# Two token tiles of a query unit share one double PSUM buffer during the query fill

## The chip, the cores and the metric

The kernel runs on one core of a Trainium2 chip. The metric is the device time of one execution in microseconds. The core's engines work side by side, each through its own queue in order: TensorE (PE, matmuls, with weight loads shown as PEld), VectorE (DVE), ScalarE (ACT), GpSimd (POOL), and SyncE (SP), which here issues every DMA. Matmul results land in PSUM, a memory of eight banks; a bank holds 512 fp32 values on each of 128 partitions.

## The reference, cut to what matters

The input x has 8 sequences of 1024 tokens with 512 features. It is normalised, and then a Performer attention block with its own MLP, and an RWKV-like feed-forward block, both work on the normalised tokens; the output is the sum of x and of both.

```python
def _phi(u, omega):
    proj = jnp.einsum('bhsk,mk->bhsm', u, omega)          # 16 heads, k = 32, m = 128
    sq = 0.5 * jnp.sum(u * u, axis=-1, keepdims=True)
    stab = jnp.max(proj, axis=-1, keepdims=True)
    return jnp.exp(proj - sq - stab) / jnp.sqrt(m) + 1e-06
...
pq = _phi(q * scale, omega)
pk = _phi(k * scale, omega)
kv = jnp.einsum('bhsm,bhsk->bhmk', pk, v)
z = jnp.sum(pk, axis=2)
num = jnp.einsum('bhsm,bhmk->bhsk', pq, kv)
den = jnp.einsum('bhsm,bhm->bhs', pq, z)
out = num / den[..., None]
h = out.transpose(0, 2, 1, 3).reshape(B, S, H * K) @ wo
...
x = layernorm(x + h);  x = layernorm(x + gelu(x @ w1 + b1) @ w2 + b2)
```

The change touches how `_phi` is computed for the queries: the products with omega, their maximum and their exponentials.

## The kernel before, in words

**Precision.** Each fp32 matrix is split into a high and a low fp16 half, and a product is made of three fp16 matmuls (`mm3`, line 139): 12 matmuls for one 128 x 512 result.

**Stages.** First the keys, values and the feed-forward block (to some 1000 us), then the queries, the attention output and the MLP. The second part runs over 64 units; a unit `(b, u)` is 512 tokens (half a sequence) times 4 heads. For each unit, one after another over neighbouring slots:

- `proj_a` (line 413) projects the queries (tile psu), ACT and DVE split the result into u, and SP stores it (ud) and transposes it. `proj_l` (line 455) loads it back as skq; `norm` (line 437) makes the squares.
- `QB` (line 631), once for each of four tiles of 128 tokens: four matmuls write the products with omega, one for each head, into a PSUM buffer pj; DVE takes the maximum (mxq) and makes the bias (biq); ACT takes four exponentials into e and casts the high half (eq); the low half is subtracted on POOL for tiles 0 and 2 and on DVE for tiles 1 and 3; SP transposes the pair into pq.
- `QD` (line 659), twice, for tiles 0 and 1 and for tiles 2 and 3: 24 matmuls with pq into acn, then three DVE steps (nm, rc, ot). `QE` (line 692) splits and transposes the result (oT).
- `O` (line 762) multiplies with wo for each 128 tokens (tile pso); `pre` (line 790) does the layer norm and SP transposes its result into x1b; `mlp1` and `mlp2` (psw, acc) are the MLP.

**The order.** Every step is put on a time axis with `at(tau, ...)`, and the program is written in the order of tau; the axis runs in units of one slot. Matmuls are chained in that order (`mm`, line 136), so PE's queue is fixed by it. The other queues are chained as well, except between tau 72.55 and 81.55: `unpin` (line 878) removes their chains and `tail_banks` (line 146) sets them again. In that stretch a planner of the framework orders ACT, DVE, POOL and SP by when their inputs are ready in its own model, and by the order of writing among those that are ready.

This stretch is the query fill. Units 0 to 7 have their QB there, one unit in each slot. `QF` (line 57) and `QDF` (line 56) place the steps of a slot: tile 0 of the unit at 0.10, tile 1 at 0.30, the first half of QD of the unit before at 0.45, tile 2 at 0.52, QD's second half at 0.75, the projection of the next unit at 0.86, tile 3 at 0.90. So tile 3 stands directly ahead of tile 0 of the next unit, with no other matmul between them unless feed-forward matmuls are placed there. Those (psk, psr, psf) are spread over the fill up to about 78.2; the O steps of block 0 stand in slots 6.5 and 6.8 after the fill's start.

**The buffers.** `open_p` (line 115) opens the PSUM pool of pj with two buffers of shape 128 x 2 x 4 x 128, two banks each, as the key stage writes two tiles at a time. `QB` takes one such buffer for each tile and uses its first half. A buffer is given out again when all that used it is done. After `tail_banks` the pool is another one (pS), with two buffers of one bank.

In the profile most rows name line 137 (the matmul helper) or line 185 (the helper of the other engines), so rows are told apart by their tiles.

Of the kernel before, what the change touches and what calls it, by code (L numbers as in the profile page):

```python
# [60 lines left out]
def block_kernel(ctx, tc, x, wq, wk, wv, wo, om3, ln1_g, ln1_b, w1, b1, w2, b2,  # L61
# [74 lines left out]
    def mm(*a, **k):  # L136
        return chained("pe", nc.tensor.matmul(*a, **k))  # L137
# [24 lines left out]
    def st(shape, dt, name, bufs=2, tag=None):  # L162
        tag = tag or name
        pool = pools["k"] if tag in KPOOL else pools["c"] if tag in CPOOL else pools["q"] if tag in QPOOL else sp
        return pool.tile(shape, dt, name=name, tag=tag, bufs=bufs)
# [4 lines left out]
    def pst(name, k):  # L170
        pool, tag, shape = P[k]
        return pool.tile(shape, F32, name=name, tag=tag)
# [49 lines left out]
    def Y(j, t):  # L222
        return 0 if j is None else (warp(j, t),)
# [404 lines left out]
        spq.dma_start(out=ff_d[bk * 4 + t], in_=r)  # L628


    def QB(b, u, t, j=None):
        if t == 0:
            qst[b, u] = []
        p = (19.12, 21.9, 24.68, 27.46)[t]
        sk, nsq = stk["q", b, u], nrm["q", b, u]
        e = st([128, 4, 128], F32, "e", 4)
        pj = pst("pj", "pj")[:, 0]
        for h in range(4):
            mm(pj[:, h, :], sk[:, h, t * 128:(t + 1) * 128], oms, start=True, stop=True)
        yield Y(j, p + 0.3)  # L640
        mx = st([128, 4], F32, "mxq", 4)
        dve.tensor_reduce(mx, pj, AX.X, ALU.max)
        yield Y(j, p + 1.05)
        bi = st([128, 4], F32, "biq", 4)
        dve.scalar_tensor_tensor(bi, mx, -1.0 / (SU * SU), nsq[:, t * 4:t * 4 + 4], ALU.mult, ALU.add)
        yield Y(j, p + 1.3)
        for h in range(4):
            act.activation(e[:, h, :], pj[:, h, :], AF.Exp, bias=bi[:, h:h + 1], scale=1.0 / (SU * SU))
        eq = st([128, 2, 4, 128], F16, "eq", 3)
        act.copy(eq[:, 0], e)  # L650
        yield Y(j, p + (3.9 if t == 0 else 3.1))
        eng = dve if QLO[t] == "v" else gps
        eng.tensor_tensor(eq[:, 1], e, eq[:, 0], ALU.subtract)
        yield Y(j, p + (5.3 if t == 0 else 4.2))
        pq = st([128, 2, 4, 128], F16, "pq", 4)
        spq.dma_start(out=pq, in_=eq.rearrange("p z h m -> p (z h) m"), transpose=True)
        qst[b, u].append(pq)
# [237 lines left out]
    for i in range(NU):  # L895
        b, u = divmod(i, 8)
# [42 lines left out]
    for i in range(NU):  # L939
        b, u = divmod(i, 8)  # L940
# [16 lines left out]
        for t in range(4):  # L957
            if j + 1 < 0:
                at(s + 1 + QF[t], QB, b, u, t)
            else:  # L960
                at(warp(j + 1, (19.12, 21.9, 24.68, 27.46)[t]), QB, b, u, t, j + 1)
# [140 lines left out]
```

## Time and profile before

| | |
|---|---|
| median of 5 runs | 2952.76 us (2950.97 to 2957.46) |
| the profiled execution, its own time | 2950.67 us |
| its span in the profile | 2948.6 us |
| PE busy | 2781.7 us (94%) |
| DVE busy | 2260.8 us (77%) |
| ACT busy | 1758.6 us (60%) |
| POOL busy | 1018.2 us (35%) |
| first and last QB matmul of the fill | 1006.44 and 1162.55 us |
| maximum of a query tile on DVE (mxq) | 0.69 us each |
| exponential of a tile and head on ACT (e) | 0.37 us each |
| landing of a pq transpose, 1100 to 1170 us | 3.2 us |

A row of the timeline holds the start, the length, the engine, the line, the operation, the tile written, the tiles read, and the number of instructions merged into the row; in brackets stands the idle time before it and what ended that. Rows of one queue overlap where the engine pipelines. A wait for several inputs is put down to the one that came last. In the table of windows each engine has its busy time and, in brackets, its number of instructions.

### The profile page before, as it was taken

Reading aid. Unit: us, or ns where it says so; the run is one execution under the profiler, and the core shown is the slowest. Engines: PE = TensorE matmul, PEld = TensorE weight load, DVE = VectorE, ACT = ScalarE, POOL = GpSimd, SP = SyncE. Lnnn points to the kernel's source line nnn. Section 1 sums busy time; section 2 is a strip of 40 time slices with the busy share of each in tenths; the row PEclk is TensorE's granted clock in tenths of the full one; section 3 lists DMA queues with packets and bytes.
Section 4 is the critical chain, followed back from the end, with each engine's and each line's share of the span. In section 5 each row is a group of like instructions: output and inputs, shape, how many; then the busy total and the mean of one; then the engine's idle time right before and its main releaser. Section 6 shows DMA issues by size and latency. Waiting matters only on the chain. (4 is left out here: it accounts for less than half of the span.)

```text
span 2948.6 us, 52107 instructions
## 1 busy us (share of the span) xinstructions
PE 2781.7 (94%) x18784; PEld 1389.2 (47%) x18784; DVE 2260.8 (77%) x4312; ACT 1758.6 (60%) x3888; POOL 1018.2 (35%) x941
## 2 busy tenths in 40 slices
PE   4999999999998896999999999999999999999996
PEld 2554445455454443444444444444444444444442
DVE  6897888889788666667778778778777777778654
ACT  5888988888888464555555455455455454554210
POOL 3464555555543432222223223223223232232111
PEclk8999999999999997999999999999999999999998
DMA  7666667666664368868777777778777777776432
GB/s 204 158 183 172 181 169 185 187 180 181 175 168 125 116 156 198 191 149 190 173 175 176 180 174 171 189 165 177 181 167 175 183 171 172 178 176 155 118 100 86
DMA packets 839348, 494.81 MB, mean 168 GB/s; under 512 B 632017, under 2 KB 718129, under 8 KB 837041
## 3 DMA queue, kind: packets, MB, share of 16 engines
q1 hardware_dynamic: 839088, 491.49, 67.0%
q8 instruction: 147, 2.41, 0.4%
q14 instruction: 113, 0.92, 0.1%
HBM read 226.95 MB, written 113.38 MB: 115 GB/s over the span
## 5 line engine op out<-in xcount | busy, mean ns | idle before, releaser
L137 PE MATMUL psw<-x1b,w1s 128*128 128x512 f16 x3072 | 695.4, 380 | 0.8 <-DVE u L185 0.8
L137 PE MATMUL acc<-w2h,gg 128*128 128x512 f16 x2048 | 647.8, 379 | 0.0
L137 PEld LDWEIGHTS <-w1s 128*128 128x128 f16 x3072 | 296.4, 98 | 344.5 <-issue 3.4
L137 PEld LDWEIGHTS <-gg 128*128 128x128 f16 x3072 | 292.8, 98 | 324.0
L185 ACT ACTIVATE g<-psw,b1t 128x512 f32<-128x512 f32 x256 | 172.6, 686 | 371.7 <-PE psw L137 362.3
L185 ACT ACTIVATE e<-pj,biq 128x128 f32<-128x128 f32 x1024 | 291.6, 369 | 162.0 <-DVE biq L185 138.3
L137 PE MATMUL acc<-w2l,gg 128*128 128x512 f16 x1024 | 387.8, 379 | 0.0
L185 ACT ACTIVATE e<-pj,bik 128x128 f32<-128x128 f32 x1024 | 287.4, 397 | 41.5 <-DVE bik L185 41.4
L185 POOL TENSOR_TENSOR eq<-e,eq 128x512 f16<-128x512 f32 x128 | 164.7, 1286 | 387.8 <-ACT eq L185 242.7
L185 DVE TENSOR_REDUCE mxq<-pj 128x4 f32<-128x512 f32 x256 | 175.7, 687 | 108.3 <-PE pj L137 107.3
L185 POOL TENSOR_TENSOR u<-ot,u 128x512 f16<-128x512 f32 x64 | 84.3, 1318 | 470.7 <-ACT u L185 431.8
L185 ACT ACTIVATE u<-psu 128x512 f16<-128x512 f32 x128 | 76.4, 597 | 206.0 <-PE psu L137 203.2
L185 DVE SCALAR_TENSOR_TENSOR gg<-g,gg 128x512 f16<-128x512 f32 x256 | 188.1, 735 | 8.8
L185 DVE TENSOR_SCALAR gg<-g 128x512 f16<-128x512 f32 x256 | 107.9, 421 | 106.7 <-ACT g L185 106.7
L137 PE MATMUL psv<-whv,xb 128*128 128x512 f16 x512 | 167.4, 389 | 19.9 <-DMA xb<-u 18.3
L185 POOL TENSOR_TENSOR e<-u 128x512 f32<-128x512 f16 x128 | 162.3, 1268 | 69.1 <-DMA u<-u 62.6
L137 PE MATMUL psu<-xb,whk 128*128 128x512 f16 x512 | 156.9, 389 | 27.3 <-DVE v L185 23.3
L185 ACT ACT_TABLE_LOAD x114 | 146.3, 1283 | 58.0 <-DVE biq L185 48.7
L185 POOL TENSOR_TENSOR xf<-xf,be 128x512 f32<-128x512 f32 x64 | 81.5, 1273 | 287.7 <-DMA xf<-in_x 168.8
L185 DVE SCALAR_TENSOR_TENSOR ekl<-e,ekh 128x1024 f16<-128x1024 f32 x128 | 171.6, 1341 | 5.1 <-ACT ekh L185 4.9
L137 PE MATMUL psf<-whfv,kx 128*128 128x512 f16 x512 | 162.5, 379 | 7.2 <-DVE v L185 2.8
L185 ACT CAST eq<-e 128x512 f16<-128x512 f32 x256 | 158.6, 621 | 16.4 <-DMA pq<-eq 9.0
(163 smaller groups left out, 5721.6 us busy)
## 6 DMA issues: line engine op xcount, KB each, us to landing
w1s<-w1d SPq DMA_DIRECT2D x256, 256.0 KB, 3.0
ud<-u SPq DMA_DIRECT2D x128, 256.0 KB, 2.2
skk<-ud SPq DMA_DIRECT2D x192, 128.0 KB, 2.8
skq<-ud SPq DMA_DIRECT2D x192, 128.0 KB, 3.2
xt<-in_x SPq DMA_DIRECT2D x64, 256.0 KB, 3.3
xnd<-xt SPq DMA_DIRECT2D x64, 256.0 KB, 2.5
xtd<-xb SPq DMA_DIRECT2D x16, 1024.0 KB, 5.3
ffd<-rsg SPq DMA_DIRECT2D x64, 256.0 KB, 2.7
```

The source lines that it names most:

```text
L137: return chained("pe", nc.tensor.matmul(*a, **k))
L185: return lambda *a, **k: chained(self.key, f(*a, **k))
```

## The change

In the fill, an even tile takes a double buffer, uses its first half and leaves the second half for the odd tile that follows. The odd tile takes that half instead of a new buffer. So tiles 0 and 1 share one buffer and tiles 2 and 3 share the other. After the fill, where a buffer has one bank only, every tile takes its own as before. The order of the program is not edited.

```diff
+    pjh = {}
+
     def QB(b, u, t, j=None):
         if t == 0:
             qst[b, u] = []
         p = (19.12, 21.9, 24.68, 27.46)[t]
         sk, nsq = stk["q", b, u], nrm["q", b, u]
         e = st([128, 4, 128], F32, "e", 4)
-        pj = pst("pj", "pj")[:, 0]
+        if t % 2 and (b, u) in pjh:
+            pj = pjh.pop((b, u))
+        else:
+            two = pst("pj", "pj")
+            pj = two[:, 0]
+            if two.shape[1] == 2:
+                pjh[b, u] = two[:, 1]
         for h in range(4):
             mm(pj[:, h, :], sk[:, h, t * 128:(t + 1) * 128], oms, start=True, stop=True)
```

## The prediction

> **What bounds the kernel now.** I read the page first: the span, the busy slices, the clock row. The tensor engine (PE) is busy 94% of the span, so only the places where it is not busy can give time back.
>
> ```profile
> span 2948.6 us, 52107 instructions
> ...
> PEclk8999999999999997999999999999999999999998
> ```
>
> The clock has one dip inside the run, in slice 16. So I split the span at the fill of the query stage. Columns: length, busy time and instructions of PE, weight load, DVE, ACT and POOL, then granted clock, DMA share, GB/s.
>
> ```profile
> 1006.00:1102.80 96.80, 94.04 (x653) 47.05 (x654) 58.22 (x111) 61.96 (x149) 33.93 (x29) 0.98 0.64 152
> 1102.80:1163.00 60.20, 28.38 (x270) 16.18 (x269) 43.53 (x99) 27.11 (x74) 20.00 (x17) 0.75 0.84 191
> 1163.00:2948.60 1785.60, 1747.61 (x11158) 855.34 (x11155) 1327.80 (x2819) 841.13 (x1722) 448.66 (x350) 0.99 0.70 166
> ```
>
> The first query tile is written at 1006.44. Up to 1102.8 the fill is dense, because FFN matmuls stand between the tiles. From 1102.8 to 1163.0 they have run out: PE is idle 60.20 - 28.38 = 31.8 us, at a clock of 0.75. After 1163.0 PE is 98% busy, so whatever moves 1163.0 moves the end. The waits of PE from 1100 to 1165 (total, times, longest):
>
> ```profile
> PE pj L137 <- ACT e L185: 17.3, 3, 7.9
> PE acn L137 <- DMA pq<-eq: 12.1, 3, 7.0
> ```
>
> The first row is what the change works on: a tile's products wait for a bank whose exponentials are not done. It is 0.59% of the span. The second row is the next wait down the same queue. The PE timeline of the last of the three rounds shows how the two lie:
>
> ```profile
> 1144.41 0.61 PE L137 MATMUL pj<-oms,skq 96*128 96x128 f16 x8
> 1152.91 0.58 PE L137 MATMUL pj<-oms,skq 96*128 96x128 f16 x4 [7.89 <-ACT e L185]
> 1153.29 0.89 PE L137 MATMUL acn<-zq,pq 128*128 128x33 f16 x24
> 1154.02 0.59 PE L137 MATMUL pj<-oms,skq 96*128 96x128 f16 x4
> 1154.70 0.50 PE L137 MATMUL acn<-zq,pq 128*128 128x33 f16 x12
> 1162.19 0.52 PE L137 MATMUL acn<-zq,pq 128*128 128x33 f16 x12 [6.98 <-DMA pq<-eq]
> 1162.55 0.59 PE L137 MATMUL pj<-oms,skq 96*128 96x128 f16 x4
> ```
>
> By the issue order of the code the eight matmuls at 1144.41 are tile 3 of unit 6 and tile 0 of unit 7; 1152.91 is tile 1, which takes the buffer that tile 3 has just filled. Then come the first half of QD of unit 6, tile 2 (1154.02), and the second half of that QD, whose last twelve matmuls wait until 1162.19 for the transposed features of **tile 3 of unit 6**, the very tile written at 1144.41. Where that latency goes, first DVE and then the SP queue:
>
> ```profile
> 1148.10 1.25 DVE L185 TENSOR_TENSOR ot<-nm,rc 128x256 f32<-128x256 f32 x1
> 1149.27 1.27 DVE L185 TENSOR_REDUCE mxq<-pj 128x4 f32<-128x512 f32 x2
> 1150.53 0.69 DVE L185 SCALAR_TENSOR_TENSOR u<-psu,u 128x512 f16<-128x512 f32 x1
> 1151.14 0.54 DVE L185 SCALAR_TENSOR_TENSOR biq<-mxq,nsqq 128x4 f32<-128x4 f32 x2
> 1153.53 0.69 DVE L185 TENSOR_REDUCE mxq<-pj 128x4 f32<-128x512 f32 x1 [1.85 <-PE pj L137]
> 1154.64 0.69 DVE L185 TENSOR_TENSOR eq<-e,eq 128x512 f16<-128x512 f32 x1
> ```
>
> ```profile
> 1153.16 0.53 SPq L185 DMA_DIRECT2D ud<-u  x1
> 1157.45 1.25 SPq L185 DMA_DIRECT2D skq<-ud  x3
> 1158.81 6.53 SPq L185 DMA_TRANSPOSE pq<-eq  x4
> ```
>
> Tile 3's maxima start at 1149.27 only, 4.25 us after its matmuls ended, because DVE has been busy without a gap since 1124.07 with the layer norm of block 0. Its low part is ready at 1155.33 (1154.64 + 0.69), but its transpose stands on SP behind the loads of skq, which wait for ud to land: 1158.81. It lands and PE goes on at 1162.19. None of these steps asks when tile 1 was written.
>
> **The change part by part.** Removed instructions: none. Added: none; the pick of the half is done while the program is written out. In the fill 8 units x 4 tiles took 32 buffers by turns, and now take 16. After the fill the buffer is one bank wide, the new branch isn't entered, and the order there is written out by hand: 0.
>
> *Tile 1 no longer waits for tile 3 of the unit before.* In the three rounds that wait is 3.25 (at 1106.62), 6.16 (at 1134.16) and 7.89 (at 1152.91): 17.3 us. *A wait is added at tile 2*: it now takes the double buffer in which tile 3 of the unit before stands, so it waits for the same exponentials. Behind it on PE stand the second half of QD, the projection of the next unit and tile 3; DVE's sums of that half wait for them. Round by round:
>
> Round 1. Tile 1 and QD (0.38 + 0.73 us to the next start) go ahead at 1103.4, and the nine O matmuls after them. The next step waits for the DMA of oT until 1113.44 before and after, as its transpose was issued at 1106.77 from a tile finished ahead of all this. So 1.71 grows to about 4.96 and the gain is 0. The long gap may cost clock. The row for that: after the 4.38 us gap that ended at 1006.44, the psr matmuls start 0.43 us apart instead of 0.22, for about eight of them, 1.7 us. Behind it lie 1.35 us of waiting for pq (until 1118.72) and 0.43 for DVE (until 1124.81), 1.78 together, which hide it; with that cover gone it costs 1.7.
>
> Round 2. Tile 1 goes from 1134.16 to about 1128.0, QD's first half to 1128.4; tile 2 waits for tile 3's exponentials until 1134.16, where before it came at 1135.27. The second half of QD still ends its wait when tile 3's transpose lands, at 1140.31: the wait of 3.82 grows by what is won. Gain 0.
>
> Round 3. Tile 1 goes at 1145.0. QD's first half then meets a wait of its own: the transpose of tile 1 of unit 6 was issued from 1146.39 on and takes some 3.2 us to land, so about 1149.6; tile 2 follows tile 3's exponentials at 1152.80 instead of 1154.02, and the end is 1162.19 as before. DVE's 1.85 us of idleness before 1153.53 goes, so tile 3's subtraction can come up to 0.29 earlier (its cast ends at 1154.35, it starts at 1154.64); the SP row at 1158.81, 3.5 us later, hides that. Gain 0.
>
> [...]
>
> *The order on DVE, ACT, POOL and SP.* Only PE is pinned between 72.55 and 81.55 on the code's time axis; the other four queues are ordered by a planner by the time at which work is ready in its own model, earlier-written work first. Tile 1's steps (a reduce and a bias on DVE, four exponentials and a cast on ACT, a subtraction on DVE, one transpose on SP, which may now pass the x1b and oT transposes and the w2 loads) become ready sooner, and QD's three DVE steps with them, so these orders can change from about 1102.8 on. The trace of before cannot show the new orders; the bounds come from its rows. Downwards: tile 3's transpose ahead of skq, 1158.81 - 1155.33 = 3.48 in round 3 and 1137.12 - 1136.54 = 0.58 in round 2; its maxima at once, 4.25 in round 3 and 1130.79 - 1128.00 = 2.79 in round 2; sum 11.1. Upwards: tile 1's maxima, bias and exponentials (0.69 + 0.15 + 1.14 = 1.98) and its transpose (1.24) put ahead of tile 3's, 3.22 a round, 9.7. A smaller unknown lies inside DVE's busy stretch: a step ot takes 0.42 alone but 1.25 at 1148.10, while POOL runs; such collisions can come or go at some 0.8 each. I take 0 for all this, the nearest row: written order puts tile 3's steps ahead of tile 1's, and DVE has the same work between 1124 and 1149 either way.
>
> Sum: 0 + 0 + 0 + 0. The profiled execution took 2950.67, its span of 2948.6 and 2.07 around it; the median shown is 2952.76, 2.09 higher. Forecast 2952.8.
>
> **The rivals.** *A, faster: the new orders shorten tile 3's way.* For it: tile 1's old lateness held SP back as well (its transpose could not be issued before 1146.39, after a subtraction at 1145.65). Against: the chain through DVE, ud and skq stands. Price: the SP parts and the maxima of round 2, 3.48 + 0.58 + 2.79 = 6.9, giving 2945.9; with all 11.1, 2941.7; the whole removed wait, 17.3, would give 2935.5.
>
> *B, slower: tile 1 is served ahead of tile 3.* Written three in a row, tile 1's reduce and exponentials can run while tile 3's cast or bias is not quite ready, and engines keep their order. Price 1.98 to 3.22 a round, 5.9 to 9.7 in all; in the middle 7.8, giving 2960.6. It decides from three full rounds on: with two it stays within 0.2%, about what a measurement of this kernel can tell from no change (5.9 us). Against: tile 3's steps are written first.
>
> *C, the change doesn't do what it says:* if the buffer were followed as a whole, tile 1 would wait for tile 0's exponentials, 1.1 us after tile 3's (a pair takes 2.17). Three rounds: up to 3.3 us, 2956.1. For it: the matmuls into kac at 964.44 wait for a read of other columns of the same bank. Against: here the halves are 512 fp32 values, a bank each.
>
> **How the numbers follow.** Forecast 0.49, A 0.24, B 0.21, C 0.06. Faster is A, 0.24; slower is B, 0.21; the forecast and C fall within 0.2%: 0.55. The range goes down to A's middle, 2944, and up to B's, 2961, which leaves out about half of A and of B, 2 in 10; the forecast alone lies in 2949 to 2957.
>
> **What would show it.** Right: tile 1 follows tile 0 on PE without a wait; the row of pj waiting for exponentials falls from 17.3 to about 7.4 (1129.1 to 1134.16 and 1150.4 to 1152.80) and stands at tile 2; acn waiting for pq grows; the first psw starts within 3 us of 1162.93; PE's idle time from 1102.8 on stays near 31.8. A shows as psw before 1157 with pq ahead of skq on SP; B as tile 3's cast behind tile 1's exponentials. The prediction fails if the orders differ enough to bring a wait on SP or ACT that no row here shows.

## The result, and the profile after

| | before | after |
|---|---|---|
| median | 2952.27 us (37 runs) | 2957.14 us (19 runs) |
| profiled span | 2948.6 us | 2955.3 us |
| from the first query tile to the first psw matmul | 156.49 us | 161.66 us |
| from there to the end of the span | 1785.67 us | 1786.07 us |

The changed kernel takes 1.0018 of the time of before, 95% interval 1.0012 to 1.0024: 4.9 us more. That is just inside the 0.2% that the forecast called no change, and yet clearly slower. The third row is worked out from the two timelines (1162.93 - 1006.44 and 1169.23 - 1007.57), the fourth from the spans. Of the 6.7 us between the two spans 5.2 lie in the query fill, 0.4 behind it, and 1.1 ahead of it, where the two programs are the same; the last section says how far figures from one profile carry.

The forecast said that tile 1 would follow tile 0 on PE without a wait. It does not. The same stretch of the PE timeline after the change, rounds 1, 2 and 3, starting each time with tile 3 of one unit and tile 0 of the next (x8), and the first psw row:

```profile
1107.13 0.61 PE L137 MATMUL pj<-oms,skq 96*128 96x128 f16 x8
1112.03 0.38 PE L137 MATMUL pj<-oms,skq 96*128 96x128 f16 x4 [4.29 <-ACT e L185]
...
1131.85 0.61 PE L137 MATMUL pj<-oms,skq 96*128 96x128 f16 x8
1143.15 0.58 PE L137 MATMUL pj<-oms,skq 96*128 96x128 f16 x4 [10.69 <-ACT e L185]
...
1156.51 0.91 PE L137 MATMUL pj<-oms,skq 96*128 96x128 f16 x8
1161.53 0.59 PE L137 MATMUL pj<-oms,skq 96*128 96x128 f16 x4 [4.12 <-ACT e L185]
...
1169.23 1.06 PE L137 MATMUL psw<-x1b,w1s 128*128 128x512 f16 x2
```

The exponentials of the pair on ACT, rounds 1 and 2:

```profile
1109.81 2.18 ACT L185 ACTIVATE e<-pj,biq 128x128 f32<-128x128 f32 x8 [1.44 <-DVE biq L185]
...
1140.94 2.16 ACT L185 ACTIVATE e<-pj,biq 128x128 f32<-128x128 f32 x8
```

Tile 1 starts at 1112.03 and 1143.15, when all eight exponentials are done (1109.81 + 2.18 = 1111.99; 1140.94 + 2.16 = 1143.10), so it waits for those of **tile 0**, the tile in the other half of its own buffer, and not for tile 3's, which end 1.1 us earlier. The list of the built program's PE queue says the same: in the fill every odd tile carries a wait on ACT, 16 of 16, and no even tile does. A pair from it:

```
14730 L137 Matmult pj_15277<-oms_266,skq_15016 128x128
14732 L137 Matmult pj_15277<-oms_266,skq_15016 128x128
14734 L137 Matmult pj_15277<-oms_266,skq_15016 128x128
14736 L137 Matmult pj_15277<-oms_266,skq_15016 128x128
14738 L137 Matmult pj_15277<-oms_266,skq_15016 128x128 [waits Activation_49]
```

The first four matmuls write tile 0's half of buffer 15277; the fifth, the first of tile 1, writes the other half and waits. The framework follows the buffer as one thing: a write to one half waits for the reads of the other.

That wait also stands in the dense part of the fill, where there was none before. PE and ACT after, unit 1:

```profile
1027.95 0.39 PE L137 MATMUL pj<-oms,skq 96*128 96x128 f16 x4
...
1034.91 0.58 PE L137 MATMUL pj<-oms,skq 96*128 96x128 f16 x4 [3.98 <-ACT e L185]
```

```profile
1031.76 0.63 ACT L185 ACTIVATE who<-wst 128x512 f16<-128x512 f32 x1 [1.27 <-DMA wst<-in_wo]
1032.30 1.03 ACT L185 CAST mx<-xm 128x1024 f16<-128x1024 f32 x1
1033.23 0.59 ACT L185 ACTIVATE kr<-psk 128x512 f32<-128x512 f32 x1
1033.72 1.13 ACT L185 ACTIVATE e<-pj,biq 128x128 f32<-128x128 f32 x4
```

Tile 0's exponentials stand on ACT behind the split of a weight (who) that is still being loaded, though DVE had their bias ready at 1029.26; tile 1 with all the FFN matmuls (of the feed-forward block) behind it waits 3.98 us for them. The waits of PE over the whole fill after the change, to be read beside the 17.3 and 12.1 of before:

```profile
PE pj L137 <- ACT e L185: 23.5, 5, 10.7
PE acn L137 <- DVE nm L185: 5.4, 2, 3.9
PE acn L137 <- DMA pq<-eq: 5.3, 3, 3.3
```

The wait that the change was to take away has grown by 6.2 us; the wait for the transposed features has shrunk by 6.8, and 5.4 of waiting for DVE are new.

### The profile page after: what moved, and what is told of

It is laid out like the page before. It is cut to its first block, busy times and chain, and to the rows that moved or that the text cites. A ratio compares the mean times of both kernels' runs of the same rounds, so it can differ in the third digit from the quotient of the medians.

```text
span 2955.3 us, 52123 instructions
## 1 busy us (share of the span) xinstructions
PE 2783.3 (94%) x18784; PEld 1389.9 (47%) x18784; DVE 2257.6 (76%) x4312; ACT 1762.1 (60%) x3888; POOL 1018.7 (34%) x941
## 5 line engine op out<-in xcount | busy, mean ns | idle before, releaser
L185 POOL TENSOR_TENSOR x<-x,bb 128x512 f32<-128x512 f32 x64 | 88.2, 1378 | 239.2 <-ACT u L185 165.6
```

What stands on the lines that cost most here:

```text
L185: return lambda *a, **k: chained(self.key, f(*a, **k))
```

## The experiments

Three theories. **W**: the loss is the wait of the odd tiles for the even tiles' exponentials, with the orders that the planner makes around it. **O**: the loss is a reordering of the other queues, above all DVE's in round 2, and a better order gives it back. **M** is the forecast's own claim, which the change as built could not test: even without any wait for a buffer the fill would not get shorter, as QD's wait takes over. The intervals of the ratios below reach some 0.09% to each side, 2.7 us (0.15% and more in the pair with the written order).

### Four buffers of one bank

```diff
     def open_q():
         early.close()
+        wide2.close()
+        ppq = proj.enter_context(tc.tile_pool(name="ppq", bufs=4, space=PSUM, side="right"))
+        P["pj"] = (ppq, "pj", [128, 1, 4, 128])
```

(`wide2` holds the pool with the two double buffers, which the key stage needs until then.)

> The key stage keeps its two double buffers; from the start of the query fill the products get four buffers of one bank, one for each tile, so that no tile waits for another tile of its own unit. Nothing is shared. If the loss of the change (+0.18%) comes from the wait of the odd tiles for the even tiles' exponentials, it is gone here: the waits of pj at 1034 and in the three rounds disappear or shrink below 3 us in all. Then the forecast's own theory is put to the test: the wait of QD for the transposed features of tile 3 takes over, and the time is that of before, 2949 to 2955 (ratio 0.999 to 1.001). If, against it, the 17.3 us of waiting were real gain: 2935 (0.994). If the loss came from tile 1 being ready sooner and the queues being reordered by that, this kernel is slower than before too, 2957 or more (1.0018).

Measured: ratio 0.9997, 0.9989 to 1.0006; median 2950.73. The waits of PE in its fill, and round 3:

```profile
PE acn L141 <- DMA pq<-eq: 16.2, 2, 9.5
PE acn L141 <- DVE nm L189: 7.8, 2, 5.0
PE pso L141 <- DMA oT<-u: 6.6, 1, 6.6
```

```profile
1144.37 0.83 PE L141 MATMUL pj<-oms,skq 96*128 96x128 f16 x12
1145.04 0.76 PE L141 MATMUL acn<-zq,pq 128*128 128x33 f16 x24
1145.65 0.38 PE L141 MATMUL pj<-oms,skq 96*128 96x128 f16 x4
1151.08 0.50 PE L141 MATMUL acn<-zq,pq 128*128 128x33 f16 x12 [5.05 <-DVE nm L189]
1158.23 0.52 PE L141 MATMUL acn<-zq,pq 128*128 128x33 f16 x12 [6.64 <-DMA pq<-eq]
```

Here four tiles do stand in a row: tile 3 of unit 6 and tiles 0 and 1 of unit 7 (x12), QD's first half, tile 2, none of them waiting. No wait of pj for exponentials is left in the fill. What took its place is 16.2 us of waiting for pq, 7.8 for DVE and 6.6 for oT. The first psw comes 155.73 us after the first query tile, against 156.49. So M holds, with the orders that the planner makes of the four buffers, which are not those of before: the whole 17.3 us of waiting can be taken away and 0.8 us of the fill is gained in this profile, less than the times can tell from nothing; their interval leaves room for 3.2 us at most.

### The change for the first four units alone, and for the last four alone

```diff
-            if two.shape[1] == 2:
+            if two.shape[1] == 2 and u < 4:      # the other run: u >= 4
```

> The change for units 0 to 3 alone, the dense part of the fill. By the two traces, the way from the first query tile to the first of the three rounds is 3.24 us longer with the change (96.32 before, 99.56 after), from a wait of 3.98 us of unit 1's tile 1 for unit 1's tile 0. If that wait does it, this kernel is slower by about 3 us, 2955.5 (1.001), and nothing is lost from 1103 on. If the loss is made by the orders in the three rounds, it is at 2952 (1.000).

> The change for units 4 to 7 alone. By the two traces the rest of the loss, 5.57 - 3.24 = 2.3 us, is made in the three rounds: 7.9 lost in round 2, where tile 3's maxima stand behind layer norm steps on DVE, and 5.8 won back. If the parts add up: 2954.5 (1.0008). If the loss is all in the dense part: 2952 (1.000). If the order in round 2 is what costs and nothing gives it back: 2957 to 2960.

Measured: first four 1.0000 (0.9990 to 1.0010), last four 1.0006 (0.9997 to 1.0016). Neither part is clear of no change, and the two sum to 0.0006 where the whole gave 0.0018; with intervals this wide that is no contradiction, but the split of the loss between the dense part and the rounds is not settled by the times. In the traces both have their waits: the first psw comes 158.80 us after the first query tile with the first four (2.3 later than before, with a wait of 3.83 in unit 1), and 160.64 with the last four (4.2 later, with a wait of 11.28 in round 2).

The traces settle more of the split than the times do. From the first query tile to round 1 the fill takes 99.56 to 101.48 us in the four profiles that have the wait there (the changed kernel, the first four, and two runs below: the wait alone, and the changed kernel with the norm behind the maxima), and 96.32 to 99.04 us in five that don't have it (the kernel before, the four buffers, the last four, and below the late load and the kernel before with the norm behind the maxima). By the means, 100.8 and 97.7, the wait costs an estimated 3 us in the dense part, as the first run's expectation said. That this run's time shows no loss is not explained; the three rounds took 57.32 us in its profile against 60.17 before, in an order of its own, but rounds of one program differ by as much (see the last section).

### The wait alone, without sharing

The four buffers again, and one edge added:

```diff
         for h in range(4):
-            mm(pj[:, h, :], sk[:, h, t * 128:(t + 1) * 128], oms, start=True, stop=True)
+            r = mm(pj[:, h, :], sk[:, h, t * 128:(t + 1) * 128], oms, start=True, stop=True)
+            if h == 0 and j is None and t % 2:
+                tc.add_manual_dep(
+                    r.ins, lastx[b, u, t - 1],      # the last exponential of tile t - 1
+                    mybir.DependencyInfo(mybir.DependencyClass.Sync, mybir.DependencyReason.DATA),
+                    reason="wait for the even tile",
+                )
```

> The four buffers of one bank of the run above, with one thing added: the first matmul of an odd tile in the fill waits for the last exponential of the even tile ahead of it. No buffer is shared, and the order of all five queues comes out instruction for instruction as with the change. If the wait, with the orders planned around it, is the whole of the loss, this is the time of the changed kernel: 2955.5 to 2959 (1.0012 to 1.0024). If sharing itself cost something (two engines on one buffer, say), it is faster than the changed kernel by that and lies at 2952 to 2954.

Measured: 1.0014, 1.0005 to 1.0022; median 2956.69. With nothing shared, this edge brings the loss back; the first psw comes 162.54 us after the first query tile. Its waits are those of the changed kernel almost to the digit:

```profile
PE pj L141 <- ACT e L189: 23.5, 4, 10.7
PE acn L141 <- DVE nm L189: 5.3, 2, 3.9
PE acn L141 <- DMA pq<-eq: 5.1, 3, 3.1
```

W is confirmed as a cause: the edge, with the orders planned around it, takes the kernel from 0.9997 to 1.0014, and the order of all five queues is that of the changed kernel. Sharing a buffer costs nothing beyond this wait that the times can show. What it would cost if PE wrote one half while ACT reads the other is not tested, as the wait keeps the two apart. What is still mixed is the wait itself and the orders planned around it.

### The wait under one fixed order

```diff
-    at(TK, unpin)
```

With the chains left on, all queues of the fill stand in the written order, once with the buffers of before and once with the shared ones.

> The kernel before, with the chains of all queues left on in the query fill, so that ACT, DVE, POOL and SP stand there in the order in which the program is written. This is the base for the next run. Against the kernel before it may go either way; the planner's order should be better, so 2953 to 2965.

> The changed kernel with the same written order on all queues. The orders of this pair are the same but for a few positions after the fill, so the two differ by the waits alone. If the wait of the odd tiles for the even tiles' exponentials costs by itself, this is 3 to 6 us (0.1 to 0.2%) slower than the run above. If the loss of the change is made by the orders that the planner chooses around the wait, above all tile 3's maxima behind the layer norm on DVE in round 2, the two agree within 2 us.

Measured: 1.0295 (1.0280 to 1.0310) and 1.0327 (1.0310 to 1.0344); medians 3039.69 and 3047.98. The written order is 87 us slower, which is a base and nothing else. Upon it the shared buffers cost 8.3 us more, where 3 to 6 was expected if the wait costs by itself. The waits of PE for exponentials, first without and then with sharing, from the two kernels' tables:

```profile
PE pj L137 <- ACT e L185: 14.4, 3, 8.8
```

```profile
PE pj L137 <- ACT e L185: 22.6, 4, 10.2
```

8.2 us more of this wait and 8.3 us more time; in the two profiles the way from the first query tile to psw is 7.5 us longer (246.36 against 238.90). That the first two figures agree to 0.1 us is chance in part, as some other waits of PE shrank at the same time (for DVE's x at pso, from 8.1 to 4.3). So the wait costs without any help from the planner. That in the planned kernels the orders hide part of it or move it elsewhere is a reading of the traces, not shown by a run.

### The order on DVE in round 2, set by hand

In the changed kernel tile 3's maxima started 5.2 us after their matmuls had begun (1131.85), behind layer norm steps:

```profile
1136.29 0.75 DVE L185 SCALAR_TENSOR_TENSOR x<-x,mvP,g 128x512 f32<-128x512 f32 x1
...
1137.09 1.28 DVE L185 TENSOR_REDUCE mxq<-pj 128x4 f32<-128x512 f32 x2
```

An edge puts the statistics of three of the four tiles of that norm behind the maxima:

```diff
-        dve.bn_stats(bst, t)
+        r = dve.bn_stats(bst, t)
+        if behind:
+            after(r.ins, behind)      # behind: the maxima of tile 3 of unit 5
```

It was run in the changed kernel and in the kernel before.

> The changed kernel with one order on DVE set by hand: the layer norm statistics of tiles 1 to 3 of block 0 stand behind the maxima of tile 3 of unit 5. In round 2 of the changed kernel those maxima started 5.2 us after their matmuls (1131.85 to 1137.09; 1127.39 to 1130.79 before) and tile 1 waited 10.69. The shared buffers and their waits stay as they are. If the loss of 4.9 us is made by that order, the maxima come some 4 us sooner, the wait of 10.69 falls to about 6.5 and the time returns to 2952 to 2954 (1.000 to 1.0006). If the loss is carried by the waits, whatever DVE does, or DVE's work as a whole ends the fill, it stays at 2955 to 2958 (1.001 to 1.002).

> The same order set by hand in the kernel before. There the maxima came 2.79 us after their matmuls had ended. If tile 3's way to its transpose is what ends a round, this is up to 2.8 us faster, 2949 (0.999); if DVE's work as a whole ends the fill, 2952 (1.000). The rival A of the forecast needed this gain.

Measured: changed kernel 1.0011 (1.0002 to 1.0019), kernel before 1.0009 (1.0000 to 1.0018). In the changed kernel the edge does what it says, and the fill is no shorter as a whole. Its maxima of tile 3 and tile 0 in round 2, tile 1 in round 2, and then tile 3 in round 3; below them tile 1's matmuls on PE in these two rounds:

```profile
1130.40 0.68 DVE L185 TENSOR_REDUCE mxq<-pj 128x4 f32<-128x512 f32 x1
1132.19 0.67 DVE L185 TENSOR_REDUCE mxq<-pj 128x4 f32<-128x512 f32 x1
1137.41 0.68 DVE L185 TENSOR_REDUCE mxq<-pj 128x4 f32<-128x512 f32 x1
...
1152.40 0.68 DVE L185 TENSOR_REDUCE mxq<-pj 128x4 f32<-128x512 f32 x1
```

```profile
1135.85 0.59 PE L137 MATMUL pj<-oms,skq 96*128 96x128 f16 x4 [5.74 <-DVE rsP L185]
...
1159.45 0.58 PE L137 MATMUL pj<-oms,skq 96*128 96x128 f16 x4 [9.74 <-ACT e L185]
```

Round 2's wait of tile 1 fell from 10.69 to 5.74, but the norm's steps moved into round 3, where it rose from 4.12 to 9.74, and the first psw came after 162.44 us, against 161.66. Of this profile's fill 101.41 us lie ahead of round 1, where the edge changes nothing (99.56 in the changed kernel), and the three rounds together took 1.1 us less. O in its plain form is not borne out: the median of 2956.97 lies where the other expectation put it. But the interval reaches down into the 1.000 to 1.0006 that O asked for, so this order may make a part of the loss. In the kernel before with the same edge the fill was 5.7 us longer (162.15), 2.7 of it ahead of round 1, and the 2.8 us of gain are not there: 0.999 lies outside the interval. In the kernel before DVE was busy without a gap from 1124.07 to 1151.68; in both runs its work is the same, and what was taken forward pushed something else back.

### The other ways out of the fill

Tiles 0 to 3 of units 4 to 7 written one behind another with four buffers, ahead of both halves of QD:

```diff
-                at(s + 1 + QF[t], QB, b, u, t)
+                at(s + 1 + (QF if i < 4 else (0.10, 0.30, 0.40, 0.42))[t], QB, b, u, t)
```

> Four buffers of one bank in the fill, and for units 4 to 7 the four tiles written one behind another: 0, 1, 2, 3 at 0.10, 0.30, 0.40, 0.42 of the slot, ahead of both halves of QD of the unit before. If the three rounds are a loop of QD waiting for tile 3 of the unit before and tile 3 standing behind that QD, this breaks the loop: tile 3 of each unit is written some 10 us sooner, and the end of the fill moves up until DVE's own work (some 43 us in the 60) ends it: 5 to 12 us faster, 2940 to 2947 (0.996 to 0.998). If the rounds are bound by DVE and SP alone: 2950 to 2953 (1.000).

Measured: 0.9992, 0.9983 to 1.0001. The loop of QD and tile 3 is broken, PE is through with QD at 1150.57, and then:

```profile
1146.27 0.50 PE L141 MATMUL acn<-zq,pq 128*128 128x33 f16 x12 [2.64 <-DVE nm L189]
1150.05 0.52 PE L141 MATMUL acn<-zq,pq 128*128 128x33 f16 x12 [3.28 <-DMA pq<-eq]
1158.82 8.12 PE L141 MATMUL psw<-x1b,w1s 128*128 128x512 f16 x24 [8.26 <-DMA x1b<-u]
```

The MLP waits for block 0's normalised tokens, which DVE now makes later: its last low half of them (u from x) is ready 152.2 us after the first query tile, 141.5 before. The fill ends after 155.08 us.

The kernel before, with the load of skq for unit 8 behind tile 3's transpose on SP:

```diff
+            if kind == "q" and (b, u) == (1, 0):
+                after(d.ins, lastp[0, 6])      # the transpose of tile 3 of unit 6
...
-            at(s + 0.32 - e, proj_l, "q", b, u)
+            at(s + (0.93 if i == 8 else 0.32 - e), proj_l, "q", b, u)
```

> The kernel before, with one thing moved: the loads of skq of unit 8 stand on SP behind the transpose of tile 3 of unit 6, which in round 3 waited behind them. The forecast put 3.48 us on that place (1158.81 to 1155.33). If SP is what ends QD's wait in round 3, the first psw comes 3.5 us sooner and the time is 2949 (0.9988). If DVE's subtraction or the landing ends it anyway, the time is that of before, 2952 (1.000).

Measured: 0.9994, 0.9985 to 1.0002. The interval holds both expectations. QD's last wait went from 6.98 to 4.56, and round 3, where the move acts, took 13.71 us from its tile 3 to psw against 18.52 before. But round 3 began after 142.61 us instead of 137.97, though the program up to there is that of before, and the first psw came after 156.32 us. So whether the 3.48 us that the forecast saw on SP can be had from that move stays open.

The four tiles in a row and the late load together, with block 0's norm written ahead of unit 6's tiles:

```diff
-                at(TQ + 7.2 + 0.02 * t, bstat, "P", n, t)
+                at(TQ + 6.91 + 0.02 * t, bstat, "P", n, t)
                 if t % 2:
-                    at(TQ + 7.21 + 0.02 * t, rstat, "P", n, t - 1)
-                at(TQ + 7.3 + 0.15 * t, pre, n, t)
+                    at(TQ + 6.92 + 0.02 * t, rstat, "P", n, t - 1)
+                at(TQ + 7.0 + 0.02 * t, pre, n, t)
```

> The four tiles in a row of the run above and the late load of skq, with one thing more: the layer norm of block 0 (the statistics, the reciprocal root, the four normalisations) is written at 6.91 to 7.06 of the axis after the fill's start instead of 7.2 to 7.75, ahead of the tiles of unit 6. In the run above PE was through with QD at 1150.57 and then waited 8.26 us for x1b. If DVE can do that norm first without making QD late, the first psw comes up to 8 us sooner, 147 to 150 us after the first query tile instead of 155.08 (156.49 before), and the time is 2944 to 2947 (0.997 to 0.998). If DVE's work as a whole ends the fill, QD becomes late by what x1b gains: 2949 to 2952 (0.999 to 1.000).

Measured: 0.9989, 0.9980 to 0.9998. It is the one version whose interval lies below 1, by 0.02%; among this many runs that is weak. Its profile does not explain a gain: psw waits 7.92 for x1b and starts after 156.26 us.

And four buffers, the late load and the norm behind the maxima:

> Four buffers of one bank in the fill, the late load of skq for unit 8 and the layer norm behind the maxima of tile 3, together. If the three gains stand side by side (0.8, 1.8 and up to 2.8 us): 2946 to 2948 (0.998 to 0.9985). If they share one cover, DVE's work: 2949 to 2951 (0.999 to 1.000).

Measured: 0.9996, 0.9987 to 1.0005. The gains don't add up; the first psw comes after 156.61 us. No version that beats both kernels beyond doubt was found.

## Why the prediction was right, and where it was wrong

The number holds: 2957.14 lies in the stated 2944 to 2961 and the ratio within the 0.2% that was called no change. That is luck in part. The road to it was wrong, the measured median lies 4.9 us on the slow side of before and just outside the 2949 to 2957 given to the forecast alone, and the range reached up to 2961 for rival B, which did not occur.

- **"Tile 1 no longer waits for tile 3 of the unit before."** True to the letter, and the step failed: a wait for tile 0 took its place, and tile 0's exponentials end after tile 3's. The 17.3 us did not fall to 7.4 but grew to 23.5. The claim that each half can be written while the other is read, because each is a bank, was made for the hardware; the framework's bookkeeping decided.
- **Rival C** is what happened, and it was given 0.06. The row that spoke for it (matmuls into kac waiting for a read of other columns of the same bank) was set aside because here the halves are whole banks. Its price of 3.3 us was too small against 4.9. It counted the three rounds and left out the dense part, taken as covered by FFN matmuls: a tile that waits on an ordered queue holds those matmuls back too (3.98 us in unit 1, an estimated 3 us of the way to round 1). It also left the planner's orders out. How much each adds to the time is not settled: the two halves of the change measured 1.0000 and 1.0006.
- **Round 1, gain 0, hidden by the wait for oT**: held. Tile 1's wait of 4.29 in the changed kernel, and its absence with four buffers, both end in the wait for oT (1.38 and 6.59). Its term for the clock was too small: behind the 6.59 us gap the fifteen O matmuls up to tile 2 took 5.90 us (1110.76 to 1116.66) against 3.25 before, 2.65 more where 1.7 was priced, and the two waits behind them, 1.78 together before, were gone.
- **Rounds 2 and 3, gain 0, the wait for tile 3's transpose grows by what is won**: held, as far as the times can tell, in the kernel where the wait really goes. There the wait for pq is 16.2 us instead of 12.1 with 7.8 for DVE beside it, and the time 0.9997. The Trainium skill, "TensorE: Matmul & The Clock Gate", section "HAM oscillation — how this bites in real kernels", reports no further gain from double-buffering PSUM in a kernel whose loop had first been rewritten so that waits on DMA no longer cooled PE at every step. The four buffers here had no gain either, at 0.9997, but with DMA waits left on PE's queue.
- **The added wait at tile 2**: not seen. Tile 2 comes behind tile 1, which by then has waited longer.
- **The orders, taken at 0, with 11.1 us downwards and 9.7 upwards**: of the downward parts two were tried. The maxima brought forward gave 1.0009 in the kernel before, so their 2.79 us of round 2 are not there; DVE gave what was won to another late step. The late load gave 0.9994, which leaves its 3.48 us of round 3 open. The sum took each delay in tile 3's way as time that could be won; with four buffers, late load and maxima together the time was 0.9996.
- **B**, tile 1 served ahead of tile 3, did not occur: on ACT tile 3 and tile 0 still come first in all three rounds.

## What to carry to other kernels

A shared buffer helps only if whoever sets the waits sees its parts as separate; look for the wait in the built program's queue before the clock is asked, and give separate buffers where it stands. A wait that heads the list may be worth nothing: name the wait that ends next on the same queue, then take the first away in full and see what takes its place. On an engine that is busy without a gap, an order that serves one step sooner makes another later, and several such moves need not add up; here they didn't.

## What was not expected of the hardware

One profile is a poor ruler for a few microseconds here. From the first psw to the end of the span the programs do the same work, yet this part took 1785.67 us in the profile before, 1786.07 after, 1786.93 with four buffers and 1793.48 with the four tiles in a row, whose profiled execution was the slowest of its eleven (2954.30, median 2949.66). Within the fill one program differs as well: the way from the first query tile to round 1 took 96.32 to 99.04 us in the five profiles without the wait there, in which the order up to round 1 is the same, and the late load's profile took 19.04 us for round 2 against 17.02 before, again in the same order. And the first query tile, ahead of which nothing differs, started between 1002.65 and 1007.57 us. The medians of the kernel before moved between 2952.0 and 2954.2 from one group of runs to another. Within the fill the granted clock fell with the idle time, to 0.50 between 1150 and 1160 us in the kernel before and with the four tiles in a row, where PE was busy for 2.2 and 1.7 of 10 us (in this order below):

```profile
1150.00:1160.00 10.00, 2.20 (x44) 2.02 (x44) 5.52 (x13) 6.49 (x21) 3.93 (x4) 0.50 0.91 177
...
1150.00:1160.00 10.00, 1.70 (x15) 0.85 (x16) 6.89 (x8) 7.37 (x16) 7.42 (x6) 0.50 0.56 125
```

So a wait there is paid once more in the matmuls behind it: in the changed kernel the twelve matmuls of a projection took 2.59 us from 1129.26 (clock 1.00 between 1120 and 1130) and 5.08 us from 1151.43, behind the waits of round 2 (clock 0.64 between 1150 and 1160).
